# Picking source rows with TensorE from the first step to the last, with the parts of x made between k and v

## The chip, the cores and the metric

The kernel runs on one core of one Trainium2 chip. The metric is device time in microseconds (us) of one launch. The kernel before has a median of 3076.03 us over 14 runs (3071.71 to 3078.97). Profiles come from one execution each, taken by the hardware profiler.

The engines are named as in the profile: PE is TensorE (PEld its weight loads), DVE is VectorE, ACT is ScalarE, POOL is GpSimd, and SP is SyncE, which here only issues DMAs.

## What is computed

The reference is one layer of a graph network with a residual and a layer norm. There are 6,250 nodes with 64 features and 206,250 edges, sorted by destination:

```python
Qh = (x @ Wq.T + bq).reshape(n, H, D)          # H = 4, D = 16
Kh = (x @ Wk.T + bk).reshape(n, H, D)
Vh = (x @ Wv.T + bv).reshape(n, H, D)
Ee = (edge_attr @ We.T + be).reshape(-1, H, D)
score = (Kh[src] * Qh[dst] * (1.0 / np.sqrt(D)) * Ee).sum(-1)
score = jnp.exp(jnp.clip(score, -5.0, 5.0))
msg = Vh[src] * score[..., None]
wV = jax.ops.segment_sum(msg, dst, num_segments=n)
x = _layernorm(x + wV.reshape(n, H * D), axis=-1)
```

Every edge needs the k and v rows of its source (a row of 128 floats at a random place of a table) and the q row of its destination (near its neighbours', since the edges are sorted).

## The kernel before

**Tiling.** 128 edges make a tile, 8 tiles a group, and 202 groups hold the 1,612 tiles. A step works on two groups; the last eight groups are a step each. That makes 105 steps: 0 to 96 with 16 tiles and 97 to 104 with 8 (the last has 4).

**Order.** The program is written out by hand under a manual schedule: each engine runs its instructions in exactly the order in which the source emits them, and waits in that order too.

**Prologue.** k and v of all nodes are computed (L320) and written to a table in HBM. Meanwhile POOL fetches rows of x for the first four groups (L230). Then q is computed in three bf16 parts (L350, L352, L353 and a helper) and written to a second table. Last, a loop over the first four groups in halves turns the fetched x rows (L375, copied by L378) and multiplies them (L380, L382, copied by L384) into k and v of these groups. The xT table (64 features, padded to 6,400 nodes) lies in SBUF for all this. After the prologue POOL has sent 32 gathers for groups 4 to 7; then a branch on a loaded value begins the main path.

**The five buffers.** A step's k and v rows stand in one of five buffers of 16 tiles. Normally a tile's rows come by one indirect DMA from the table (L402, sent by POOL). The gathers for step s + 4 are emitted in step s, behind the message product L619; their buffer is the one that L619 of step s - 1 read last.

**One step s**, in short: squares and relu on ACT make one-hot columns of the destinations for step s + 1 (L555, L572, L577); sums of step s - 1 (L638); products k * q * e (L602, L603), their sum and exponential (L609, L611, L612); the message (L619); its split in three bf16 parts, where PE subtracts between two ACT copies (L622, L630, L632); the one-hot matrix of the next step (L585) and its queries (L595).

**Picking.** For two tiles of most steps the rows aren't gathered. PE picks them instead. The table of x, split in three bf16 parts, lies in SBUF as 50 blocks of 128 rows (`parts`). For a tile, ACT subtracts 50 * column from the source numbers (L466), PE turns that (L471), DVE compares it with the block numbers in two halves of 25 blocks (L481, two "hots" a tile), and PE multiplies each of the 50 one-hot blocks with its block of parts (L491, 50 matmuls a tile). DVE sums the three parts (L498); PE turns the result (L505, copied by L507) and multiplies it by the k and v weights (L513, L515); ACT copies it into the buffer (L516). The pick of step p spans steps p and p + 1 and serves step p + 2, of which it fills the last two tiles. Here p runs from `M0` = 4 to `LAST` = 94: 91 picks, 182 tiles.

**Making the parts.** In steps 0 to 3 the function `table_parts` loads x in seven blocks on SP's queue (L448) and splits it on ACT and DVE (L450, L451, L456 to L458), two blocks a step.

**Row fetches.** Every sixth step from 12 to 96 ("rowed") has one further tile whose rows SP fetches one by one (L544) into a tile that ACT copies (L548).

**Count.** Of the 1,612 tiles, 32 come from the prologue, 182 are picked, 15 are fetched by SP and 1,383 gathered by L402.

Of the kernel before, what the change touches and what calls it, by code (L numbers as in the profile page):

```python
# [37 lines left out]
CB = 10  # L38
KVB = 5
XG = 4  # L40
TB = 8
M0 = 4
PAD = N
SPARE = N + 1
TABLES = 4
# [4 lines left out]
def tiles_of(g):  # L50
    return min(G, T - g * G)
# [9 lines left out]

LAST = NS - 8 - 3


def picks_in(s):
    return M0 <= s <= LAST

# [33 lines left out]
def tile_gnn(ctx: ExitStack, tc: tile.TileContext, x, xT, wT, bias, beT, weT, eT, src, dst, dst_rows,  # L103
# [50 lines left out]
    be_p = consts.tile([3, G, C], BF16, name="be_p")  # L154
    wkv = consts.tile([P, 2, 2 * C], F32, name="wkv")
    bkv_p = consts.tile([3, G // 2, 2 * C], BF16, name="bkv_p")
    minus_b = consts.tile([P, P], BF16, name="minus_b")

    acc = consts.tile([P, RING, 4, C], F32, name="acc")
# [24 lines left out]
    with tc.tile_pool(name="nodes", bufs=1) as nodes, \  # L184
# [182 lines left out]
            fetch_queries(g)  # L367


        for g in range(XG):  # L370
            for h in range(2):
                tp = npsum.tile([P, 2, P], F32, name="tp", bufs=2)
                for u in range(2):
                    j = 4 * h + 2 * u
                    nc.tensor.transpose(tp[:, u, :],  # L375
                                        XS[g][:, j:j + 2, :].rearrange("p j c -> p (j c)"), ident)
                xe = nodes.tile([P, 2, P], F32, name="xe", bufs=2)
                nc.scalar.activation(xe, tp, AF.Copy)  # L378
                pv = npsum.tile([P, 4, 2 * C], F32, name="pv", bufs=2)
                nc.tensor.matmul(pv, ones_b, bkv_p, start=True, stop=False, skip_group_check=True)  # L380
                for u in range(2):
                    nc.tensor.matmul(pv[:, 2 * u:2 * u + 2, :], xe[:, u, :], wkv, start=False,  # L382
                                     stop=u == 1, skip_group_check=True)
                nc.scalar.activation(kv_of(g)[:, 4 * h:4 * h + 4, :], pv, AF.Copy)  # L384

    def edge_values(pe, et, n):

# [6 lines left out]
    def keys(t0):  # L394

        n = min(KEYS, T - t0)
        nc.vector.tensor_scalar(key_i[:, :n], dst_i[:, t0:t0 + n], P - 1, None, op0=OP.bitwise_and)
        nc.vector.tensor_copy(key[:, t0:t0 + n], key_i[:, :n, None].to_broadcast([P, n, 2]))

    def gather_kv(g, j):  # L400
        t = g * G + j
        nc.gpsimd.indirect_dma_start(  # L402
            out=kv_of(g)[:, j, :], out_offset=None, in_=kv_tab[:, :],
            in_offset=bass.IndirectOffsetOnAxis(ap=src_i[:, t:t + 1], axis=0))

    for g in range(XG, 2 * KVB - 2):
        for j in range(G):
            gather_kv(g, j)

    rv = nc.values_load(n_wide[0:1, 0:1], min_val=0, max_val=NR2 * 4)  # L410

    with tc.If(rv == 0) as branch:

        with tc.tile_pool(name="work", bufs=2) as work, \
# [11 lines left out]
            parts = accp.tile([P, NB, 3, C], BF16, name="parts")  # L426
            nc.vector.memset(parts, 0.0)
            NX = N // NB
            x_v = x.rearrange("(p b) c -> p b c", p=NX)
            n_picks = LAST - M0 + 1  # L430
            src_f = accp.tile([P, n_picks, 2], F32, name="src_f")
            t0 = (M0 + 3) * 2 * G - 2
            for i in range(2):
                nc.vector.tensor_copy(src_f[:, :, i],
                                      src_i[:, t0 + i:t0 + i + 2 * G * (n_picks - 1) + 1:2 * G])
            pick = fixed.tile([P, 4 * P], F32, name="pick")
            rows3 = pick[:, :6 * C].rearrange("p (k i c) -> p k i c", k=2, i=3)
            HOT, FAR, X = {}, {}, {}
# [2 lines left out]

                return ap.rearrange("p (a b) -> p a b", b=2)

            def table_parts(b):

                n = min(TB, NB - b)
                raw = work.tile([P, TB, C], F32, name="raw", bufs=1)
                nc.sync.dma_start(raw[:NX, :n], x_v[:, b:b + n, :])  # L448
                rest = pick[:NX, :n * C].rearrange("p (b c) -> p b c", b=n)
                nc.scalar.activation(rest, raw[:NX, :n], AF.Copy)  # L450
                nc.scalar.activation(parts[:NX, b:b + n, 0], raw[:NX, :n], AF.Copy)  # L451
                return rest

            def table_parts_rest(b, rest):
                n = min(TB, NB - b)
                nc.vector.tensor_sub(rest, rest, parts[:NX, b:b + n, 0])  # L456
                nc.scalar.activation(parts[:NX, b:b + n, 1], rest, AF.Copy)
                nc.vector.tensor_sub(parts[:NX, b:b + n, 2], rest, parts[:NX, b:b + n, 1])  # L458

            def sources(s, i):  # L460

                if picks_in(s):
                    FAR[s, i] = work.tile([P, P], BF16, name="far")
                    nc.scalar.activation(FAR[s, i], row50, AF.Identity,  # L466
                                         bias=src_f[:, s - M0, i:i + 1], scale=-1.0)

            def sources_turned(s, i):
                if picks_in(s):  # L470
# [39 lines left out]
            def picked_kv(s):  # L510
                if picks_in(s):
                    xe, kv = X.pop(s)
                    nc.tensor.matmul(kv, ones_b, bkv_p[:, :2], start=True, stop=False,  # L513
                                     skip_group_check=True)
                    nc.tensor.matmul(kv, xe, wkv, start=False, stop=True, skip_group_check=True)  # L515
                    nc.scalar.activation(kvs[(s + 2) % KVB][:, 2 * G - 2:, :], kv, AF.Copy)  # L516

            def gather(s):
                for g in groups_of(s):
                    for j in range(tiles_of(g)):  # L520
                        if is_rowed(s) and (g - STEPS[s][0]) * G + j == COLUMN:
                            continue
                        if not picks_in(s - 2) or g == STEPS[s][0] or j < G - 2:
                            gather_kv(g, j)

            RS, RK = {}, {}
# [53 lines left out]
            def onehot_edges(s):  # L580

                n, t0 = tiles_in(s), STEPS[s][0] * G
                OH[s] = work.tile([P, 2 * G, P], BF16, name="of")
                shape = [P, n, P // 2, 2]
                nc.vector.tensor_tensor(OH[s].rearrange("p t (a c) -> p t a c", c=2)[:, :n],  # L585
                                        pairs(col)[:, None].to_broadcast(shape),
                                        key[:, t0:t0 + n, None, :].to_broadcast(shape),
                                        op=OP.is_equal)
# [109 lines left out]
                                               op0=OP.mult, op1=OP.add)  # L698

            closed, scaled, normed = 0, 0, 0  # L700
            keys(0)
            for k, g in enumerate(groups_of(0)):
                onehot_rows(g, spread(g))
# [1 line left out]
                edges(0, k)  # L705
            queries(0)
            onehot_edges(0)
            for s in range(NS):
                more = s + 1 < NS
                for g in groups_of(s):  # L710
# [9 lines left out]
                    onehot_rows_rest(nexts[0])  # L720
                if s:
                    sums(s - 1)
                sources_turned(s, 1)
                sources_turned(s + 1, 0)
                if nexts[1:]:
                    onehot_rows(nexts[1], spread(nexts[1]))
                making = [b for b in range(s * 2 * TB, (s + 1) * 2 * TB, TB) if b < NB]
                if making:
                    rest = table_parts(making[0])
                prod = products(s)  # L730
                picked(s - 1)
                if more:
                    edges(s + 1, 0)
                picks(s, 0, 0)
# [5 lines left out]
                msg = message(s, score)  # L740
                if s + KVB - 1 < NS:
                    gather(s + KVB - 1)
                picked_turned(s - 1)
                if nexts[1:]:
                    edges(s + 1, 1)
                minus(s, msg, 0)
                hots(s, 1, 0)
                picks(s, 0, 1)
                minus(s, msg, 1)
                picked_kv(s - 1)  # L750
                if not more:

                    close(B - 2)
                    spreads(B - 2)
                hots(s, 1, 1)
                picks(s, 1, 0)
                sources(s + 1, 1)
                sources(s + 2, 0)
                if s + 1 < NS:
                    rows_fetched(s + 1)  # L760
                if more:
# [21 lines left out]
                for i, b in enumerate(making):  # L783
                    if i:
                        rest = table_parts(b)
                    table_parts_rest(b, rest)
            assert normed == B - 2
            sums(NS - 1)
            roots(B - 2, B - 1)
# [9 lines left out]
    with branch.Else():  # L799

        sums = [dram.tile([NR, C], F32, name=f"sums{i}") for i in range(TABLES)]
        with tc.tile_pool(name="gconsts", bufs=1) as gc, \
                tc.tile_pool(name="gloads", bufs=3) as loads, \
                tc.tile_pool(name="ggath", bufs=4) as gath, \
# [28 lines left out]
            def gather(g, j):  # L833
                if j == 0:
                    Q[g] = gath.tile([P, G, C], F32, name="gq")
                t = g * G + j
                if g >= 2 * KVB - 2:
# [125 lines left out]
```

## Time and profile before

| What | us |
|---|---|
| median of 14 runs | 3076.03 |
| the profiled execution | 3077.2 |
| its span, first to last instruction | 3075.2 |
| POOL busy in L402 (1,383 gathers of 0.946) | 1308.5 |
| PE busy in the picks, L491 (9,100 of 0.115 in the mean) | 1046.0 |
| DVE busy in the hots, L481 (364 of 1.818 and a pipelined start) | 651.3 |
| PE waits before the queries, L595, for nothing that the profile shows | 562.7 |
| mean granted TensorE clock | 0.783 |

How to read it: the time of one execution is its span and some 2 us around it. Busy time is an engine's work, not its share of what sets the end; no engine is busy for more than two thirds of the span. "Wait" lines name the waiting engine and line, who released it, the total in us, the count and the longest. "Remote" means that a semaphore changed with no instruction ending just before. A gather's duration is POOL's own work for it; the rows land later. Gathers that follow each other start 1.25 us apart.

### The profile page before, as it was taken

What the parts mean: (1) busy time and instruction counts of PE and PEld (TensorE: products, weight loads), DVE (VectorE), ACT (ScalarE), POOL (GpSimd) and SP (SyncE); (2) the same over time, 40 slices, a digit from 0 to 9 for tenths busy, and PEclk for the clock granted to TensorE, in tenths of its full rate; (3) what the DMA queues carried; (4) which work ended last, traced back from release to release, by engine and by line L of the source; (5) the groups of instructions that cost most, each with busy time, mean ns of one, the idle gap of its engine ahead of it and who ended that gap; (6) DMA issues with size and microseconds to landing.
All of it is one profiled execution on the core that took longest, in us unless ns stands there. A gap on an engine that the chain in (4) does not pass through costs nothing. (4 is left out here: it accounts for less than half of the span.)

```text
span 3075.2 us, 44286 instructions
## 1 busy us (share of the span) xinstructions
PE 1987.2 (65%) x15751; PEld 1552.6 (50%) x15751; DVE 1503.4 (49%) x1695; ACT 918.7 (30%) x1328; POOL 1340.6 (44%) x1427
## 2 busy tenths in 40 slices
PE   4555766657676666667576766666576766667675
PEld 4334545545454555545454555545454545545553
DVE  3234545545454545545454545445454545455554
ACT  2242323323232323223232322323232323223334
POOL 5455444343444444353444444353434444453342
PEclk9967878778787878777777778777777878777885
DMA  5222112121212112221211111121212122121121
GB/s 145 71 77 60 53 45 56 44 58 44 55 45 54 53 46 52 53 58 44 56 51 48 53 46 48 51 57 44 60 46 56 45 54 54 46 58 42 51 58 31
DMA packets 109971, 166.71 MB, mean 54 GB/s; under 512 B 69197, under 2 KB 71453, under 8 KB 109627
## 3 DMA queue, kind: packets, MB, share of 16 engines
q0 software_dynamic: 45280, 91.78, 11.8%
q1 hardware_dynamic: 64074, 71.01, 8.0%
q8 instruction: 125, 2.05, 0.3%
q10 hardware_dynamic: 384, 1.00, 0.2%
q14 instruction: 108, 0.88, 0.1%
HBM read 156.33 MB, written 7.33 MB: 53 GB/s over the span
## 5 line engine op out<-in xcount | busy, mean ns | idle before, releaser
L402 POOL DMA_INDIRECT kv<-kv_tab,src_i x1383 | 1308.5, 946 | 1677.7 <-DVE pq L619 1237.3
L491 PE MATMUL pick<-parts,hot 128*128 128x192 bf16 x9100 | 1046.0, 275 | 267.4 <-issue 266.6
L491 PEld LDWEIGHTS <-hot 128*128 128x128 bf16 x9100 | 889.4, 109 | 398.3 <-issue 342.8
L481 DVE TENSOR_TENSOR hot<-small,block 128x3200 bf16<-128x3200 bf16 x364 | 651.3, 1818 | 298.5 <-remote 258.1
L595 PE MATMUL pq<-qw,to 126*128 126x64 bf16 x1612 | 164.0, 221 | 663.6 <-issue 562.7
L572 ACT ACTIVATE to<-pb,minus_row 126x1024 bf16<-126x1024 f32 x202 | 223.1, 1104 | 996.5 <-PE pb L555 941.5
L602 DVE TENSOR_TENSOR prod<-kv,pq 128x1024 f32<-128x1024 f32 (+2 forms) x105 | 123.7, 1178 | 779.6 <-PE pq L595 387.5
L595 PEld LDWEIGHTS <-to 126*128 126x128 bf16 x1612 | 108.0, 113 | 739.9 <-issue 736.5
L632 ACT ACTIVATE msg<-pq 128x1024 bf16<-128x1024 f32 (+2 forms) x210 | 207.8, 990 | 771.5 <-remote 522.6
L391 PE MATMUL pe<-we_sb,et 128*128 128x128 f32 x1612 | 247.6, 299 | 0.0
L391 PEld LDWEIGHTS pe<-we_sb,et 128*128 128x128 f32 x1612 | 207.3, 201 | 54.1 <-issue 48.3
L577 ACT ACTIVATE to<-to,one_p 126x1024 bf16<-126x1024 bf16 x202 | 230.6, 1142 | 3.5
L609 DVE TENSOR_REDUCE small<-prod 128x64 f32<-128x1024 f32 (+2 forms) x105 | 124.4, 1185 | 188.1 <-PE small L471 148.3
L638 PEld LDWEIGHTS <-of 128*128 128x128 bf16 x1612 | 156.6, 108 | 49.9 <-issue 41.0
L638 PE MATMUL small<-msg,of 128*128 128x192 bf16 x1612 | 170.9, 265 | 0.5 <-ACT msg L632 0.5
L630 PE MATMUL pq<-msg,minus_b 128*128 128x512 bf16 x404 | 128.5, 398 | 59.0 <-ACT msg L622 45.3
L555 PE MATMUL pb<-key_rows,ident_b 112*128 112x512 bf16 x403 | 154.2, 472 | 4.9 <-ACT to L572 2.6
L622 ACT ACTIVATE msg<-pq 128x1024 bf16<-128x1024 f32 (+2 forms) x105 | 103.9, 990 | 95.9 <-DVE pq L619 95.9
L603 DVE TENSOR_TENSOR prod<-prod,pe 128x1024 f32<-128x1024 f32 (+2 forms) x105 | 123.6, 1177 | 3.6
L619 DVE TENSOR_TENSOR pq<-kv,small 128x1024 f32<-128x1024 f32 (+2 forms) x105 | 123.5, 1176 | 1.4 <-ACT small L612 1.4
L585 DVE TENSOR_TENSOR of<-small,key 128x2048 bf16<-128x2048 bf16 (+2 forms) x105 | 123.2, 1173 | 0.3
L498 DVE TENSOR_REDUCE xp<-pick 128x128 f32<-128x384 f32 x91 | 50.7, 558 | 98.8 <-PE pick L491 98.3
(129 smaller groups left out, 992.1 us busy)
## 6 DMA issues: line engine op xcount, KB each, us to landing
et<-in_eT SPq DMA_DIRECT2D x100, 512.0 KB
rk<-kv_tab SPq DMA_DIRECT2D x1920, 0.5 KB
kv<-kv_tab,src_i POOLq DMA_INDIRECT x1383
qw<-q_tab SPq DMA_DIRECT2D x202, 15.8 KB
kv_tab<-kv_sb SPq DMA_DIRECT2D x5, 640.0 KB
q_tab<-q SPq DMA_DIRECT2D x5, 480.0 KB
acc<-in_x SPq DMA_DIRECT2D x48, 32.0 KB
out<-y SPq DMA_DIRECT2D x48, 32.0 KB
```

Of the source, the lines that this page charges most:

```text
L391: nc.tensor.matmul(pe[:, 2 * u:2 * u + 2, :], et[:, u, :], we_sb, start=False, stop=u == n // 2 - 1, skip_group_check=True)
L402: nc.gpsimd.indirect_dma_start(out=kv_of(g)[:, j, :], out_offset=None, in_=kv_tab[:, :], in_offset=bass.IndirectOffsetOnAxis(ap=src_i[:, t ...
L481: nc.vector.tensor_tensor(HOT[s, i, h].rearrange("p b (a c) -> p b a c", c=2), pairs(from_b[i])[:, None].to_broadcast(shape), block2[:, bl ...
L491: nc.tensor.matmul(rows3[:, i], hot[:, k, :], parts[:, b], start=b == 0, stop=b == NB - 1)
L555: nc.tensor.matmul(pb[:, b:b + 4, :], ident_b[:NR2, g // 2:g // 2 + 1].to_broadcast([NR2, P]), key_rows[:, g % 2, b * P:(b + 4) * P], star ...
L572: nc.scalar.activation(TO[g][:, :n, :], pb[:3 * W, :n, :], AF.Square, bias=minus_row3[:3 * W])
L577: nc.scalar.activation(TO[g][:, :n, :], TO[g][:, :n, :], AF.Relu, bias=one_p[:3 * W], scale=-1.0)
L595: nc.tensor.matmul(PQ[s][:, (g - STEPS[s][0]) * G + j, :], TO[g][:, j, :], QW[g], start=j == 0, stop=j == tiles_of(g) - 1, skip_group_chec ...
L609: nc.vector.tensor_reduce(score, prod[:, :n, :].rearrange("p g (h d) -> p g h d", h=H), axis=AX.X, op=OP.add)
L630: nc.tensor.matmul(msg[:, lo:hi, :], minus_b, M3[s][:, lo:hi, i, :], start=False, stop=True, skip_group_check=True)
L632: nc.scalar.activation(M3[s][:, :n, i + 1, :], msg[:, :n, :], AF.Copy)
L638: nc.tensor.matmul(PA[s], OH[s][:, j, :], M3[s][:, j], start=j == 0, stop=j == n - 1)
```

## The change

The parts of x are now made in the prologue, out of the xT table in SBUF, by PE transposes between the turned x rows and the k and v of the first groups. No step makes parts any more, and the loads of x for them and the memset are gone. Picks run from step 0 on (`PAIRS`, `TARGET`): steps 0 to 96 pick two tiles each for the step two later. Picks 97, 99 and 101 are spread over two steps each, one tile in each step, and serve steps 100, 102 and 104, each a step of one group, whose last two tiles they fill. So 200 tiles are to be picked, and L402's gathers go down by 18. Step 0's first hots are made before the loop.

The core of the diff:

```diff
-TB = 8
-M0 = 4
+TB = 4
-LAST = NS - 8 - 3
-def picks_in(s):
-    return M0 <= s <= LAST
+LAST = NS - 8 - 1
+PAIRS = [*range(LAST + 1), *range(LAST + 1, NS - 3, 2)]
+TARGET = {p: p + (2 if p <= LAST else 3) for p in PAIRS}
+def picks_in(p):
+    return p in PAIRS
+def second_of(s):
+    return s if s <= LAST else s - 1 if s - 1 in PAIRS else None
+def is_picked(g, j):
+    s = max(s for s in range(NS) if STEPS[s][0] <= g)
+    return s in TARGET.values() and g == groups_of(s)[-1] and j >= tiles_of(g) - 2
...
+        def parts_of_x(b):
+            n = min(TB, NB - b)
+            px = npsum.tile([P, 2, 2 * C], F32, name="ps").rearrange("p i (j c) -> p (i j) c", j=2)
+            px = px[:, :n]
+            for u in range(n):
+                nc.tensor.transpose(px[:, u, :], xT_sb[:C, (b + u) * P:(b + u + 1) * P],
+                                    ident[:C, :C])
+            nc.scalar.activation(parts[:, b:b + n, 0], px, AF.Copy)
+            nc.vector.tensor_sub(px, px, parts[:, b:b + n, 0])
+            halves.append((px, b, n))
+        def rest_of_x():
+            px, b, n = halves.pop(0)
+            nc.scalar.activation(parts[:, b:b + n, 1], px, AF.Copy)
+            nc.vector.tensor_sub(parts[:, b:b + n, 2], px, parts[:, b:b + n, 1])
+        order = [(g, h) for g in range(XG) for h in range(2)]
+        blocks = list(range(0, NB, TB))
+        xe = x_turned(*order[0])
+        for i, gh in enumerate(order):
+            following = x_turned(*order[i + 1]) if i + 1 < len(order) else None
+            for b in blocks[2 * i:2 * i + 2]:
+                parts_of_x(b)
+            first_kv(*gh, xe)
+            xe = following
+            while halves:
+                rest_of_x()
...
     for g in range(XG, 2 * KVB - 2):
         for j in range(G):
-            gather_kv(g, j)
+            if not is_picked(g, j):
+                gather_kv(g, j)
...
-                    nc.scalar.activation(kvs[(s + 2) % KVB][:, 2 * G - 2:, :], kv, AF.Copy)
+                    n = tiles_in(TARGET[s])
+                    nc.scalar.activation(kvs[TARGET[s] % KVB][:, n - 2:n, :], kv, AF.Copy)
...
+            sources(0, 0)
+            sources_turned(0, 0)
             keys(0)
...
             onehot_edges(0)
+            sources(0, 1)
+            sources(1, 0)
+            for h in range(2):
+                hots(0, 0, h)
             for s in range(NS):
...
-                sources_turned(s, 1)
+                sources_turned(second_of(s), 1)
                 sources_turned(s + 1, 0)
...
-                making = [b for b in range(s * 2 * TB, (s + 1) * 2 * TB, TB) if b < NB]
-                if making:
-                    rest = table_parts(making[0])
                 prod = products(s)
-                picked(s - 1)
+                picked(second_of(s - 1))
...
-                picked_turned(s - 1)
+                picked_turned(second_of(s - 1))
...
-                hots(s, 1, 0)
+                hots(second_of(s), 1, 0)
                 picks(s, 0, 1)
                 minus(s, msg, 1)
-                picked_kv(s - 1)
+                picked_kv(second_of(s - 1))
...
-                hots(s, 1, 1)
-                picks(s, 1, 0)
-                sources(s + 1, 1)
+                hots(second_of(s), 1, 1)
+                picks(second_of(s), 1, 0)
+                sources(second_of(s + 1), 1)
...
-                picks(s, 1, 1)
+                picks(second_of(s), 1, 1)
```

`x_turned(g, h)` and `first_kv(g, h, xe)` are the two halves of the old loop over the first groups, unchanged. The rest of the diff sets `src_f` (the source numbers of the picked tiles) for all picks, removes `table_parts`, and lets the other branch, which doesn't run here, gather the tiles that are now left out ahead of it.

More of the change, by code (lines that the diff above doesn't have):

```diff
@@ L156, in tile_gnn @@
     bkv_p = consts.tile([3, G // 2, 2 * C], BF16, name="bkv_p")
+    parts = consts.tile([P, NB, 3, C], BF16, name="parts")
     minus_b = consts.tile([P, P], BF16, name="minus_b")
@@ L367, in tile_gnn, with x_turned @@
             fetch_queries(g)
[L370 to L384, printed above, removed]
+        def x_turned(g, h):
+            tp = npsum.tile([P, 2, P], F32, name="tp", bufs=2)
+            for u in range(2):
+                j = 4 * h + 2 * u
+                nc.tensor.transpose(tp[:, u, :], XS[g][:, j:j + 2, :].rearrange("p j c -> p (j c)"),
+                                    ident)
+            xe = nodes.tile([P, 2, P], F32, name="xe", bufs=2)
+            nc.scalar.activation(xe, tp, AF.Copy)
+            return xe
@@ new lines, in first_kv @@
+        def first_kv(g, h, xe):
+            pv = npsum.tile([P, 4, 2 * C], F32, name="pv", bufs=2)
+            nc.tensor.matmul(pv, ones_b, bkv_p, start=True, stop=False, skip_group_check=True)
+            for u in range(2):
+                nc.tensor.matmul(pv[:, 2 * u:2 * u + 2, :], xe[:, u, :], wkv, start=False,
+                                 stop=u == 1, skip_group_check=True)
+            nc.scalar.activation(kv_of(g)[:, 4 * h:4 * h + 4, :], pv, AF.Copy)
+        halves = []
+        def parts_of_x(b):
[8 more added lines that the diff above has]
+            halves.append((px, b, n))
@@ L424, in tile_gnn @@
             nc.tensor.transpose(col, row_b[:, 0:1].to_broadcast([P, P]), ident_b)
[L426 to L432, printed above, removed]
-            for i in range(2):
-                nc.vector.tensor_copy(src_f[:, :, i],
-                                      src_i[:, t0 + i:t0 + i + 2 * G * (n_picks - 1) + 1:2 * G])
+            src_f = accp.tile([P, PAIRS[-1] + 1, 2], F32, name="src_f")
+            full = NS - 8 - 2
+            for i in range(2):
+                t0 = 3 * 2 * G - 2 + i
+                nc.vector.tensor_copy(src_f[:, :full, i],
+                                      src_i[:, t0:t0 + 2 * G * (full - 1) + 1:2 * G])
+            for p in PAIRS[full:]:
+                t0 = STEPS[TARGET[p]][0] * G + tiles_in(TARGET[p]) - 2
+                nc.vector.tensor_copy(src_f[:, p], src_i[:, t0:t0 + 2])
             pick = fixed.tile([P, 4 * P], F32, name="pick")
@@ L442, in pairs @@
                 return ap.rearrange("p (a b) -> p a b", b=2)
[L444 to L458, printed above, removed]
             def sources(s, i):
@@ L466, in sources @@
                     nc.scalar.activation(FAR[s, i], row50, AF.Identity,
-                                         bias=src_f[:, s - M0, i:i + 1], scale=-1.0)
+                                         bias=src_f[:, s, i:i + 1], scale=-1.0)
             def sources_turned(s, i):
@@ L522, in gather @@
                             continue
-                        if not picks_in(s - 2) or g == STEPS[s][0] or j < G - 2:
+                        if not is_picked(g, j):
                             gather_kv(g, j)
@@ L782, in tile_gnn @@
                             normed += 1
[L783 to L786, printed above, removed]
             assert normed == B - 2
@@ L803, in tile_gnn @@
                 tc.tile_pool(name="gloads", bufs=3) as loads, \
-                tc.tile_pool(name="ggath", bufs=4) as gath, \
+                tc.tile_pool(name="ggath", bufs=3) as gath, \
                 tc.tile_pool(name="gwork", bufs=2) as work, \
@@ L836, in gather @@
                 t = g * G + j
-                if g >= 2 * KVB - 2:
+                if g >= 2 * KVB - 2 or is_picked(g, j):
                     gather_kv(g, j)
```

## The prediction

> **What bounds the kernel now.** I read the wait table first, since no engine is busy for more than 65% of the span.
>
> ```profile
> PE 1987.2 (65%) x15751; PEld 1552.6 (50%) x15751; DVE 1503.4 (49%) x1695; ACT 918.7 (30%) x1328; POOL 1340.6 (44%) x1427
> ...
> POOL kv L402 <- DVE pq L619: 1237.3, 98, 14.6
> ACT msg L632 <- remote: 522.6, 53, 15.8
> DVE hot L481 <- remote: 258.1, 50, 9.6
> ```
>
> Two things are to be seen. POOL's row gathers (L402) idle 1237.3 us until the message product L619 of a step frees a kv buffer: each step sends one burst of gathers right behind its L619. And ACT and DVE wait long for a semaphore that no instruction ended just before ("remote"): what they wait for is PE. The timeline of one step, at 1004 us, shows why (start, duration, engine, line; in brackets the idle time before and what ended it).
>
> ```profile
> 1004.09 0.95 POOL L402 DMA_INDIRECT kv<-kv_tab,src_i  x1 [12.76 <-DVE pq L619]
> ...
> 1007.88 0.59 PE L630 MATMUL pq<-msg,minus_b 128*128 128x512 bf16 x2
> ...
> 1016.85 1.02 ACT L632 ACTIVATE msg<-pq 128x1024 bf16<-128x1024 f32 x1 [9.81 <-remote]
> ...
> 1020.36 0.94 POOL L402 DMA_INDIRECT kv<-kv_tab,src_i  x1 [0.30 <-issue]
> ...
> 1024.33 4.19 PE L491 MATMUL pick<-parts,hot 128*128 128x192 bf16 x25
> 1024.61 1.22 DVE L602 TENSOR_TENSOR prod<-kv,pq 128x1024 f32<-128x1024 f32 x1 [6.62 <-PE pq L595]
> ...
> 1035.00 0.94 POOL L402 DMA_INDIRECT kv<-kv_tab,src_i  x1 [13.70 <-DVE pq L619]
> ```
>
> PE's L630 is recorded at 1007.88, yet ACT, which needs it alone, starts at 1016.85. While the 14 gathers run (17.2 us) PE crawls; the work left over, 13.70 us from the burst's end to the next, sets the step: 17.2 + 13.7 = 30.9. So a step is worth its burst plus whatever PE, DVE and ACT still have to do behind it. That second part I read from a table by stage, cut at the starts of L619 (width, busy us of PE, PEld, DVE, ACT, POOL, then clock, DMA share, GB/s).
>
> ```profile
> 181.40:205.95 24.55, 12.58 (x58) 7.94 (x58) 9.60 (x14) 11.20 (x15) 13.23 (x14) 0.50 0.30 81
> 229.50:253.00 23.50, 12.85 (x77) 8.42 (x76) 11.83 (x17) 8.57 (x12) 13.23 (x14) 0.65 0.26 65
> 283.20:313.80 30.60, 19.59 (x167) 15.70 (x165) 15.44 (x19) 8.62 (x13) 13.24 (x14) 0.78 0.19 50
> 2921.60:2945.50 23.90, 19.39 (x167) 15.47 (x165) 14.45 (x14) 8.22 (x12) 7.58 (x8) 0.86 0.17 47
> 2966.80:2982.10 15.30, 8.80 (x58) 5.87 (x58) 6.85 (x9) 6.68 (x10) 7.56 (x8) 0.78 0.26 70
> 3031.90:3040.40 8.50, 6.37 (x30) 3.80 (x30) 4.81 (x12) 4.24 (x6) 0.00 (x0) 0.50 0.07 15
> ```
>
> With 14 gathers, a step without picking takes 23.5 to 24.6 and one with it 30.6. With 8 gathers they take 15.3 and 23.9. So **picking costs 6 to 8.6 us in a step**, and a gather less saves (30.6 - 23.9)/6 = 1.1 us. Two tiles picked save 2.2 and cost three times that. The change adds picking to the stages that are cheap now.
>
> **The prologue.** Removed from the first four steps: seven loads on SP's queue, the memset of the parts, and the making with 35 short instructions (five for each of seven blocks); in step 0 two of them (L450, L451, 0.59 + 0.62) stand before the exponential on ACT: -1.1. Added between k and v: 50 transposes on PE, 26 copies on ACT (some 0.38 each, by L378's 128x256) and 26 DVE subtractions. The loop there is PE's alone:
>
> ```profile
> 113.37 2.79 PE L350 MATMUL ps<-w_sb,xT_sb 65*128 65x64 f32 x12 [2.44 <-DVE q L341]
> ...
> 119.32 0.63 PE L375 MATMUL tp<-ident,xs 128*128 128x128 f32 x2
> 119.89 0.60 PE L380 MATMUL pv<-bkv_p,ones_b 3*128 3x512 bf16 x1
> 120.49 2.07 PE L382 MATMUL pv<-wkv,xe 128*128 128x256 f32 x4
> ```
>
> Eight rounds of 3.0 us, PE without a gap, so the transposes add their whole time; ACT and DVE, with under 3 us a round, hide behind. A transpose of 64 columns lies between a 64-wide float matmul pass (2.79/12 = 0.23) and a 128-wide transpose (0.63/2 = 0.32): I take 0.27, 50 of them 13.5. If PE left idle time they would cost nothing; it leaves none. The next to be late is step 0, whose spreads stand behind the loop on PE. Against this, the burst at 67 to 107 us has 28 gathers in place of 32. The q matmuls (L350) crawl under it and run freely again only at 112: -4 x 1.25 = -5.0. The two new hots and the first FAR before step 0 lie behind the 4.06 us that the memset (L427) frees on DVE. Sum: 13.5 - 5.0 - 1.1 = **+7.4**; from 0 (transposes at 0.23, half of them in gaps) to +27, if the transposes, which read xT_sb as L350 does, crawl as it did for the 20 us of the burst that runs beside the loop.
>
> **The first four steps.** From L619 of step 0 to that of step 4 the trace has 26.7 + 24.5 + 23.6 + 23.5 = 98.3. Each becomes a picking step: four L481 of 1.82 on DVE, 100 pairs on PE, the reduction L498 between the products and the scores (its 0.56 and a wait for the last pick, 98.3/82 = 1.2, with L609 queued behind), two L466 and L507, L516 on ACT with the next step's squares (L572) queued behind. Rather than add these, I take what a step with all of them lasts, 30.1 (L619 of step 4 starts at 253.0, of step 91 at 2870.2: 2617.2/87): 4 x 30.1 - 98.3 = **+22.1**. Bounds: -2.5 (all hidden, and two gathers less in the first burst), +26 (31.1, the longest usual step). I stay with the steady row, since step 4, the first that picks, already takes 30.2 under the same loads.
>
> **The last steps.** L619 of steps 92 to 100 starts at 2897.7, 2921.6, 2945.5, 2966.8, 2982.1, 2995.1, 3003.7, 3023.3 and 3031.9, then every 8.6 us. Bursts for steps 97 and 98 lose two gathers: 2 x -2.2. Step 95 begins to pick, so the period before its L619 becomes 23.9 in place of 21.3 (+2.6). The next two, 15.4 and 13.0, become picking periods: + 8.6 - 2.2 and + 8.6. Then come single-group steps of 8.6. Picks 97, 99 and 101 spread over two steps each, 50 pairs a step, half of 8.6: 4.3 for each of steps 99 to 102. One oddity: for step 97 the function second_of returns 96, which was finished in step 96, so tile two of 96 is picked **again**, and its reduction and kv again in step 98; the instruction order of the changed kernel has 10,050 pick matmuls where 100 pairs of tiles need 10,000. So step 97 does a whole pick, +8.6. Step 98 has half a pick, but its 19.6 hold a stall behind 16 gathers in a row (the products at 3018.63 idled 7.37), which longer steps spread: +2. Sum: -4.4 + 2.6 + 6.4 + 8.6 + 8.6 + 2 + 17.2 = **+41**. Bounds: +15 if the half picks fit into PE's idle time (8.5 - 6.4 = 2.1 a step), +55 if each costs as much as a half at the low clock: 50 pairs of 4.19/25 = 8.4.
>
> The row 25 pairs in 4.19 has a twin of 2.23 at 1001.81, at granted clocks of 0.50 and 1.00; the tail stands at 0.50. The Trainium skill, TensorE: Matmul & The Clock Gate (Part 1: The HAM clock gate), has the clock full after some 3.4 us of dense work and half after an idle window: by it the picks warm the tail, and an estimate is 4.5 in place of 8.4 a half step.
>
> **Sum:** 7.4 + 22.1 + 41 = 70.5 on the span of 3075.2: 3146; the profiled run, 3077.2 with what lies around, lies 1.2 over the median 3076.0. Forecast **3146**.
>
> **Rivals.** (1) *The prologue crawls* under the burst: +20, 3166. For it: L350's groups of four took 9 us there; against: L375 to L382 ran under a burst without a delay. (2) *Half picks hide* in the short steps, 41 becomes 15: 3120. For: PE has idle time there; against: a picking step's DVE and PE order puts hots and picks between L619 and the products. (3) *Bursts alone decide*, picks are free: each gather less is worth 1.25 us of POOL; four of the 18 are in the prologue's sum, so 3076 + 7.4 - 14 x 1.25 = 3066, **faster**. It decides if a pick leaves under 2.5 us behind its burst. For: picks overlap the burst in part, and rare 13-gather steps last 27.5, 3 us less than those of 14. Against: 23.5 beside 30.6 at equal gathers. The Trainium skill, SBUF — State Buffer (Who interferes with whom), says that DMA never contends with a compute engine and that PE waits on no one; by it PE would not crawl, and a pick's cost would be its 100 pairs alone. The row at 1016.85 differs, and the row decides. (4) *The change does not do what it says:* the repeat of 96 is such a case and is in the sum; without it 3137.
>
> **How the numbers follow.** Forecast 0.65, rival 1 0.15, rival 2 0.13, rival 3 0.05, and 0.02 that it comes out level. All but the last two are slower: 0.93. 0.2%, some 6 us, is what a measurement here tells from no change. The range reaches down to a free prologue with first steps and tail of +15 each, 3076 + 30 = 3106, and up to a crawling prologue (27) with first steps of 24 and a tail of 50: 3177.
>
> **What would show it.** L619 of step 0 near 162 in place of 154.7; then four periods near 30; steady periods unchanged; periods of about 21 before step 97, 13 after it; clock above 0.5 in the tail. Wrong if the first four periods stay under 27, or the single-group steps stay near 9.

## The result, and the profile after

The changed kernel takes 3112.71 us (median of 6 runs, 3107.48 to 3119.07) against 3076.69 for the kernel before in the same comparison: ratio 1.0116, 95% interval 1.0106 to 1.0126. It is 36 us slower; the forecast was 70 us slower (3146), so the sign and the range held, and the forecast rise was about twice the measured one. The profiled execution has a span of 3111.0, 35.8 more than before.

Where the 35.8 went is read from the table by stage. The first fence is the kernel before, the second the changed one; both are cut at the starts of the message product (L619 before, L650 after) of steps 0, 4 and 91. Columns: stretch, width, busy us of PE, PEld, DVE, ACT and POOL (with instructions), granted clock, DMA share, GB/s.

```profile
0.00:154.75 154.75, 83.17 (x311) 64.93 (x311) 46.15 (x134) 37.98 (x103) 77.53 (x92) 1.00 0.37 107
154.75:253.00 98.25, 50.76 (x262) 32.95 (x261) 40.11 (x51) 41.43 (x55) 54.85 (x58) 0.63 0.28 76
253.00:2870.20 2617.20, 1719.74 (x14252) 1359.58 (x14252) 1311.98 (x1348) 761.52 (x1063) 1139.15 (x1204) 0.78 0.19 51
```

```profile
0.00:156.41 156.41, 88.76 (x360) 70.14 (x361) 55.51 (x165) 45.53 (x130) 71.88 (x86) 1.00 0.36 105
156.41:275.40 118.99, 81.08 (x671) 64.42 (x671) 58.22 (x55) 34.72 (x47) 52.84 (x56) 0.80 0.18 46
275.40:2892.69 2617.29, 1721.35 (x14269) 1363.43 (x14267) 1312.11 (x1348) 761.88 (x1065) 1136.23 (x1204) 0.78 0.19 51
```

What remains to the end is 3075.2 - 2870.2 = 205.0 before and 3111.0 - 2892.7 = 218.3 after. So:

| Stage | predicted | measured |
|---|---|---|
| prologue, to the message of step 0 | +7.4 | +1.7 |
| first four steps | +22.1 | +20.7 |
| steady steps 4 to 90 | 0 | +0.1 |
| step 91 to the end | +41 | +13.3 |
| sum | +70.5 | +35.8 |

The wait table of the changed kernel (waiting engine and line, released by what; total, count, longest; three of its lines) has the same two signs as before: POOL waits for the message, and ACT and DVE wait for a PE whose recorded work ended long ago.

```profile
POOL kv L448 <- DVE pq L650: 1280.7, 99, 22.7
...
ACT msg L663 <- remote: 555.1, 58, 13.7
...
DVE hot L511 <- remote: 271.4, 53, 10.9
```

**The prologue** in the timeline, two lines of the kernel before (the first and the last matmuls of its loop):

```profile
116.22 0.69 PE L375 MATMUL tp<-ident,xs 128*128 128x128 f32 x2
...
138.69 2.07 PE L382 MATMUL pv<-wkv,xe 128*128 128x256 f32 x4
```

and the same places of the changed kernel, with the new transposes between them:

```profile
110.05 1.12 PE L388 MATMUL tp<-ident,xs 128*128 128x128 f32 x4
...
111.09 1.11 PE L409 MATMUL ps<-ident,xT_sb 64*128 64x64 f32 x8
...
115.11 1.11 PE L409 MATMUL ps<-ident,xT_sb 64*128 64x64 f32 x8
...
140.22 2.08 PE L398 MATMUL pv<-wkv,xe 128*128 128x256 f32 x4
```

The loop begins 6.2 us earlier, behind a burst that has four gathers less (5.0 was predicted). Eight transposes take 1.11, so one takes 0.139 where the prediction took 0.27; a round goes from 3.03 to 4.01. The loop lasts 32.3 in place of 24.5; some 1.5 of these 7.7 us are idle time of PE around the last two transposes (136.51, below), not the transposes' own. From the loop's end to the message it is 14.1 in place of 14.0: -6.17 + 7.71 + 0.12 = +1.66.

Behind the loop two changes cancel. The message of step 0 no longer waits for the two copies that made parts on ACT, but PE's first step work (L586) starts 1.88 us behind the loop in place of 0.74, since the first FAR and its transpose now stand ahead of it:

```profile
136.51 0.45 PE L409 MATMUL ps<-ident,xT_sb 64*128 64x64 f32 x2 [1.27 <-issue]
...
143.64 0.40 ACT L496 ACTIVATE far<-row,src_f 128x128 bf16<-128x128 f32 x1 [0.71 <-DVE key_i L443]
144.10 0.29 PE L501 MATMUL small<-ident_b,far 128*128 128x128 bf16 x1 [0.86 <-ACT far L496]
144.18 1.06 PE L586 MATMUL pb<-key_rows,ident_b 112*128 112x512 bf16 x2
```

**The tail** by steps 92, 93, 94, 97, 99, 100 and 101, cut at L650 (same columns):

```profile
2920.38:2938.94 18.56, 16.12 (x167) 13.41 (x165) 15.21 (x17) 8.54 (x13) 5.67 (x6) 1.00 0.20 53
2938.94:2959.04 20.10, 17.70 (x167) 14.78 (x165) 14.48 (x14) 8.53 (x13) 5.66 (x6) 0.92 0.19 49
2959.04:2981.28 22.24, 18.82 (x164) 15.58 (x162) 15.30 (x17) 8.64 (x13) 7.56 (x8) 0.85 0.18 49
...
3017.10:3032.19 15.09, 12.54 (x130) 10.73 (x128) 8.23 (x13) 5.31 (x10) 5.66 (x6) 1.00 0.24 64
...
3049.20:3058.24 9.04, 7.73 (x73) 5.97 (x71) 4.89 (x13) 5.27 (x10) 1.88 (x2) 1.00 0.19 54
3058.24:3071.70 13.46, 11.41 (x94) 9.66 (x94) 12.17 (x18) 4.14 (x6) 0.00 (x0) 0.75 0.05 10
3071.70:3080.73 9.03, 7.65 (x72) 5.86 (x70) 4.87 (x12) 4.98 (x9) 0.00 (x0) 1.00 0.07 15
```

Three things are to be seen. Steps 92 and 93, with 6 gathers in place of 8, last 18.6 and 20.1 in place of 23.9 and 23.9: a gather less is worth 1.9 to 2.7 us here, not 1.1. In the kernel before, in the step of the prediction's timeline whose burst begins at 1004.09, PE first pauses for nothing that the profile shows 7.1 us into the burst:

```profile
1011.18 0.34 PE L491 MATMUL pick<-parts,hot 128*128 128x192 bf16 x2 [0.48 <-issue]
```

Six gathers last 7.2 us and eight 9.7, so a burst of six is over about when PE begins to fall behind. That fits the gain; no run tests it by itself.

Second, the granted clock is 0.75 to 1.00 in steps 97 and 99 to 101, where before it was 0.50 to 0.54 from step 97 on. The eight edge matmuls of such a step, before and after:

```profile
3038.97 2.08 PE L391 MATMUL pe<-we_sb,et 128*128 128x128 f32 x8
...
3056.30 1.16 PE L437 MATMUL pe<-we_sb,et 128*128 128x128 f32 x8
```

At full clock a step with half a pick takes 9.03, hardly more than a step without one at half clock (8.56). Third, steps 99 and 101 make no hots; step 100 makes four, and DVE is busy for 12.2 of its 13.5 us.

### The profile page after: what moved, and what is told of

It is laid out like the page before. It is cut to its first block, busy times and chain, and to the rows that moved or that the text cites. A ratio compares the mean times of both kernels' runs of the same rounds, so it can differ in the third digit from the quotient of the medians.

```text
span 3111.0 us, 46506 instructions
## 1 busy us (share of the span) xinstructions
PE 2061.3 (66%) x16810; PEld 1636.7 (53%) x16810; DVE 1571.8 (51%) x1759; ACT 926.0 (30%) x1372; POOL 1320.4 (42%) x1409
## 5 line engine op out<-in xcount | busy, mean ns | idle before, releaser
L448 POOL DMA_INDIRECT kv<-kv_tab,src_i x1365 | 1288.1, 944 | 1721.2 <-DVE pq L650 1280.7
L521 PE MATMUL pick<-parts,hot 128*128 128x192 bf16 x10050 | 1141.3, 274 | 292.0 <-issue 291.3
L521 PEld LDWEIGHTS <-hot 128*128 128x128 bf16 x10050 | 976.8, 109 | 429.9 <-issue 367.7
L511 DVE TENSOR_TENSOR hot<-small,block 128x3200 bf16<-128x3200 bf16 x402 | 718.8, 1817 | 293.8 <-remote 271.4
L663 ACT ACTIVATE msg<-pq 128x1024 bf16<-128x1024 f32 (+2 forms) x210 | 207.6, 989 | 768.8 <-remote 555.1
L437 PE MATMUL pe<-we_sb,et 128*128 128x128 f32 x1612 | 236.9, 291 | 0.0
L437 PEld LDWEIGHTS pe<-we_sb,et 128*128 128x128 f32 x1612 | 198.0, 193 | 46.3 <-issue 43.0
L586 PE MATMUL pb<-key_rows,ident_b 112*128 112x512 bf16 x403 | 148.8, 457 | 1.5 <-ACT to L603 1.0
L650 DVE TENSOR_TENSOR pq<-kv,small 128x1024 f32<-128x1024 f32 (+2 forms) x105 | 123.5, 1176 | 0.3 <-ACT small L643 0.3
```

Of the source, the lines that this page charges most:

```text
L437: nc.tensor.matmul(pe[:, 2 * u:2 * u + 2, :], et[:, u, :], we_sb, start=False, stop=u == n // 2 - 1, skip_group_check=True)
L448: nc.gpsimd.indirect_dma_start(out=kv_of(g)[:, j, :], out_offset=None, in_=kv_tab[:, :], in_offset=bass.IndirectOffsetOnAxis(ap=src_i[:, t ...
L511: nc.vector.tensor_tensor(HOT[s, i, h].rearrange("p b (a c) -> p b a c", c=2), pairs(from_b[i])[:, None].to_broadcast(shape), block2[:, bl ...
L521: nc.tensor.matmul(rows3[:, i], hot[:, k, :], parts[:, b], start=b == 0, stop=b == NB - 1)
L586: nc.tensor.matmul(pb[:, b:b + 4, :], ident_b[:NR2, g // 2:g // 2 + 1].to_broadcast([NR2, P]), key_rows[:, g % 2, b * P:(b + 4) * P], star ...
L663: nc.scalar.activation(M3[s][:, :n, i + 1, :], msg[:, :n, :], AF.Copy)
```

## The experiments

Each kernel is compared with the kernel before on the same chip. The runs went to four chips, and this matters: on chips 13 and 15 the kernel before takes 3095 and 3096 us, on chips 0 and 3 it takes 1790 and 1793. Ratios, not times, are compared between chips of one kind. The unaltered changed kernel did not run on chip 13; e4, which differs from it by 2 to 4 us in one step, is the nearest there.

### e1: no picks at all

```diff
-PAIRS = [*range(LAST + 1), *range(LAST + 1, NS - 3, 2)]
+PAIRS = []
...
-            for b in blocks[2 * i:2 * i + 2]:
-                parts_of_x(b)
```

> No tile is picked and no parts are made: 1,565 gathers instead of 1,365, no hots, no picks. Theory: a step lasts its burst of gathers plus what PE, DVE and ACT still do behind it, 6.9 us without picking and 13.7 with it (rows of the kernel before). A step of 16 gathers then lasts 20.0 + 6.7 = 26.7 in place of 30.1, as step 0 of the kernel before did (26.66), a step with 15 about 25.4; 87 steady steps save some 87 x 3.6 = 310 us, the first four and the tail some 20 more: about 2780 us. Rival 'bursts alone decide': 200 gathers more at 1.25 us make it slower than after, 3113 + 250 = 3360. A middle result (near 3000) would mean that a longer burst holds PE back by more than its 1.25 us a gather.

Measured on chip 13: 2758.21 us, ratio 0.8914 (0.8899 to 0.8929). Two of its steps in the table by stage, cut at its message product:

```profile
281.25:308.02 26.77, 13.05 (x58) 8.00 (x58) 7.88 (x13) 7.70 (x9) 15.09 (x16) 0.56 0.21 62
1716.24:1743.06 26.82, 12.71 (x58) 7.71 (x58) 7.89 (x14) 7.91 (x10) 15.10 (x16) 0.56 0.21 61
```

Sixteen gathers and 26.8 us, the 26.7 of "burst plus 6.7". This is the reasoning of the prediction tested far from where it was read: picking two tiles costs 30.1 - 26.7 = 3.4 us a step more than gathering them (3.6 by the means of steps 4 to 90 on this chip, 26.6 here and 30.2 in e3). The rival "bursts alone decide" (3360) is out on this chip.

### e2, e3, e4: one part of the change undone

e2 gathers the tiles that steps 0 to 3 would pick, e3 those of the picks from 95 on, e4 picks the second tile of 96 once:

```diff
-PAIRS = [*range(LAST + 1), *range(LAST + 1, NS - 3, 2)]
+PAIRS = [*range(4, LAST + 1), *range(LAST + 1, NS - 3, 2)]     # e2
+PAIRS = [*range(LAST - 1)]                                     # e3
...
-    return s if s <= LAST else s - 1 if s - 1 in PAIRS else None
+    return s if s <= LAST else s - 1 if s - 1 > LAST and s - 1 in PAIRS else None   # e4
```

> The changed kernel with the picks of steps 0 to 3 left out (their 8 tiles are gathered), all else as in after. Stage theory: the first four steps cost 119.0 us in after and 98.3 before, so undoing them gives back 20 us or a little more, since nothing makes parts in them now: 3113 - 21 = 3092, range 3085 to 3096. Rival 'the loss sits elsewhere and is only seen here' (parts in the prologue delay the first steps through queues): 3108 to 3113.

Measured on chip 13: ratio 1.0069 (1.0053 to 1.0086). From after's 1.0116 that is 0.47% or 14.5 us (12.6 against e4 on the same chip), less than the 20 expected and outside the range that was given. The table by stage of e2, cut at L650 of steps 0 and 4, shows both halves of it:

```profile
0.00:163.05 163.05, 88.36 (x357) 69.88 (x358) 52.24 (x164) 44.30 (x127) 77.34 (x92) 1.00 0.34 104
163.05:260.46 97.41, 50.56 (x265) 33.01 (x265) 31.76 (x37) 32.27 (x36) 54.73 (x58) 0.61 0.20 57
```

In e3 and e4, on the same chip, step 0 reaches its message at 159.80 and 158.44, and the four steps last 120.0 and 120.3. So four steps without picks save 22.7, and with the four gathers that come back into the prologue the message comes 3.3 to 4.6 later. The expectation had left those out. The rest of the shortfall sits where the edit changes nothing: from step 4 to 91 e2's trace has 2635.6 us and e4's 2632.0, and behind that 221.8 and 216.5. That part is not explained by the stage theory.

> The changed kernel with picks 95, 96, 97, 99 and 101 left out (their ten tiles are gathered). Stage theory: from L650 of step 91 to the end after lasts 218.3 us and before 205.0, so undoing gives back 13.4: 3113 - 13 = 3099.5, range 3096 to 3102. Rival of the prediction (the tail costs 41): 3072.

Measured on chip 13: ratio 1.0084 (1.0067 to 1.0100), 0.32% or 10 us below after, a little less than the 13 expected. From L650 of step 91 to the end e3 has 206.7 us, against 216.5 in e4 and 218.3 in after. The stage theory holds; the 41 of the prediction does not. Steps 92 and 93 of e3, with 8 gathers again, last 23.5 and 23.7; those of e4, with 6, 20.2 and 18.6: the gain of the shorter bursts is seen on this chip too. The same last steps as in after took 221.8 us in e2 and 219.8 in e9, so 2 or 3 us in a single trace carry little.

> The changed kernel with the second tile of step 96 picked once (step 97 does half a pick, step 98 none of the sums, turns and products of it). The prediction's theory: the repeat costs +8.6 in step 97 and up to 2 behind it: 3104. Trace theory: steps 96 to 98 last 18.88, 15.09 and 17.01 in after against 13.00, 8.56, 19.63 before, +9.8 together, of which half a pick in step 97 must stay; half of step 97's +6.5 goes: 3109.5. Rival 'repeat hidden': 3113, no change.

Measured on chip 13: ratio 1.0117 (1.0100 to 1.0134): no difference from after that this can tell. In its trace step 97 lasts 13.04 in place of 15.09 (15.2 in e2, 16.7 in e9). By the traces the repeated pick of 96 costs 2 to 4 us, not the 8.6 to 10.6 of the expectation's first theory; the total can't tell it from nothing.

### e5 to e8: rests between the gathers

What holds PE back during a burst? Three theories: PE lives on a store of instructions that fills only between gathers; PE needs a fixed time without gathers; gathers simply take time in proportion. Short iotas on POOL, which write a tile that nothing reads, make rests; e5 to e7 are e1 with them, e8 is the changed kernel with them.

```diff
+            sent = [0]
+            idle = accp.tile([P, 512], I32, name="idle")
...
             def gather(s):
+                sent[0] = 0
...
                             gather_kv(g, j)
+                            sent[0] += 1
+                            if s < NS - 8 and sent[0] % 8 == 0:      # e6: 4, e7 and e8: 1
+                                for _ in range(4):                  # e6, e7 and e8: 1
+                                    nc.gpsimd.iota(idle, pattern=[[1, 512]], base=0,    # e7, e8: 256
+                                                   channel_multiplier=0)
```

> e1 (no picks), and in each step of two groups POOL rests after 8 and after 16 gathers: four iotas of 512 numbers, an estimate of 2 to 3 us (the 224-wide iota took 0.32). In e1 a step is 26.75 us: 20.0 of gathers and 6.75 behind them. Theory 'store': PE has some 55 instructions in store when a burst begins, which are done after 3 us (the trace of after), and then hardly any reach it until the burst ends; a rest fills the store again. Then work for 55 instructions moves from behind the burst into it: 20 + 2.5 + some 3 behind = 25 to 26 a step, 2758 - 97 x 1.2 = about 2640 to 2700. Theory 'silence': PE needs its 6.75 us without gathers anywhere: the rest counts as part of them, no change, 2750 to 2770. Theory 'proportion': rests only delay the gathers: + 2.5 a rest in the middle of each step, 2758 + 97 x 2.5 = 3000.

> e1, with one iota of 512 numbers (an estimate of 0.6 us) after every fourth gather. 'Store', if a rest of 0.6 us is long enough for the store to fill: three refills of 55 instructions cover all that a step without picking has (some 120): 20 + 2 + 1 to 2 behind it = 23 to 24, about 2450. 'Silence': 2750 to 2770. 'Proportion': 2758 + 97 x 1.8 = 2930.

> e1, with an iota of 256 numbers (an estimate of 0.35 us) after every gather, so that the same rest is spread finest: 16 x 0.35 = 5.6 us a step. 'Store': if a rest of 0.35 us lets ten or more instructions through, PE is never held and the step is the gathers with their rests, 16 x 1.6 = 25.6 or less: about 2650; if such a rest is too short to let any through, 26.75 + 5.6 = 32.3: about 3290. 'Silence': the 5.6 count, 2750 to 2770. 'Proportion': 3290.

> The changed kernel itself with the same iota of 256 after every gather of the steps of two groups. A step is 17.2 + 13.0 = 30.1 us there; it has some 330 PE instructions. 'Store' with rests that let instructions through: 14 x 1.6 = 22.4 of gathers, under which PE goes on, so that a step is 23 to 26 us: 2550 to 2750 in all. Rests too short, or 'proportion': 14 x 0.35 = 4.9 a step more, about 3590. 'Silence': 3110 to 3130.

Measured: 2419.33, 2175.63, 2362.77 and 2102.41 us, ratios 1.3515, 1.2154, 1.3201 and 1.1751. They tell nothing about the three theories, because they ran on chip 0, where the kernel before takes 1789.95 us. There PE isn't held back: in the wait table of e8 no engine waits for "remote" at all, where after has 555.1, 271.4, 197.8 and 126.6 us in its four largest such lines. With PE free, POOL sends gather after gather, and rests only lengthen that row (proportion). So the comparison up to here holds for one kind of chip only.

### e9 and e10: the changed kernel again, and five stretches in one kernel

> The changed kernel once more, unaltered, beside the kernel before on this call's chip. Runs e5 to e8 had a chip on which the kernel before takes 1790 us in place of 3076 to 3095. There 1,383 gathers of 1.25 us make 1729 us, so that POOL's gathers would be the bound, and the third rival of the prediction ('bursts alone decide') would hold: 18 gathers less are worth 22 us, ratio 0.987 (0.98 to 0.995). On a chip on which the kernel before takes some 3080 us, picking costs 3.4 us a step more than gathering its tiles, and the ratio is that of the first comparison, 1.011 to 1.013.

Measured on chip 15: 3135.85 against 3095.91 us, ratio 1.0130 (1.0113 to 1.0147). The first comparison holds on another chip of the kind that takes some 3080 us for the kernel before.

e10 puts the rests into one kernel so that either kind of chip answers:

```diff
-PAIRS = [*range(LAST + 1), *range(LAST + 1, NS - 3, 2)]
+PAIRS = [*range(61), *range(LAST - 1, LAST + 1), *range(LAST + 1, NS - 3, 2)]
...
+            def rest(s, k):
+                n = (256 if 27 <= s < 46 else
+                     2048 if 46 <= s < 65 and k == 7 else
+                     512 if 65 <= s < 83 and k % 4 == 0 else 0)
+                if n:
+                    nc.gpsimd.iota(idle[:, :n], pattern=[[1, n]], base=0, channel_multiplier=0)
```

> One kernel with five stretches (numbers of the steps that hold them fully): A, steps 6 to 20, as in after; B, 24 to 38, an iota of 256 after each gather (0.36 us of POOL, a gather and its rest took 1.48 in e8); C, 43 to 55, one iota of 2,048 numbers (some 2 us) after the seventh gather; D, 63 to 76, no picks and an iota of 512 (0.57 us) after each fourth of 16 gathers; E, 80 to 90, no picks and no rests. Steps on a chip where the kernel before takes some 3080 us: A 30.1 and E 26.7 by every theory. 'Store' (PE's store of instructions fills in each rest): B 22 to 26, C 27 to 28.5, D 21.8 to 24. 'Silence' (rests count toward the 13.0 or 6.7 us that PE needs without gathers): B 30.1, C 30.1, D 26.7. 'Proportion' (rests only delay): B 33.5, C 32.2, D 28.5. On a chip where it takes 1790 us PE isn't held, and every stretch is POOL's gathers with their rests: A 17.3, B 20.7, C 19.5, D 21.7 (as in e6), E 20.0.

Measured on chip 15: 2889.21 us, ratio 0.9332 (0.9313 to 0.9351). The table by stage of e10, cut at its message product so that the rows are the stretches A to E (15, 15, 13, 14 and 11 steps):

```profile
345.16:796.78 451.62, 292.46 (x2465) 233.94 (x2463) 224.44 (x227) 130.01 (x183) 195.48 (x207) 0.78 0.17 50
880.69:1277.29 396.60, 312.06 (x2462) 232.91 (x2462) 229.96 (x250) 133.21 (x186) 269.86 (x414) 0.86 0.20 59
1384.49:1738.44 353.95, 272.42 (x2125) 212.45 (x2123) 193.91 (x196) 113.54 (x159) 193.12 (x192) 0.82 0.19 56
1938.26:2310.18 371.92, 145.48 (x812) 92.59 (x812) 108.13 (x162) 110.40 (x118) 240.64 (x276) 0.61 0.22 63
2388.73:2682.13 293.40, 133.04 (x638) 83.84 (x638) 81.27 (x110) 85.19 (x91) 165.27 (x175) 0.57 0.21 61
```

Divided by their steps: A 30.1, B 26.4, C 27.2, D 26.6, E 26.7. In B and C POOL does more than in A (the same gathers and the rests), and the step is 3.7 and 2.9 us **shorter**. "Proportion" (33.5 and 32.2) and "silence" (30.1) fall there; "store" (22 to 26 and 27 to 28.5) is met in C and missed by 0.4 in B. The timeline of a step of C shows what the rest does (start, duration, engine, line; in brackets the idle time before and what ended it):

```profile
1498.40 0.94 POOL L448 DMA_INDIRECT kv<-kv_tab,src_i  x1 [0.30 <-issue]
1499.35 1.85 POOL L567 IOTA idle<- 128x2048 int32 x1
1500.29 1.02 ACT L675 ACTIVATE msg<-pq 128x1024 bf16<-128x1024 f32 x1 [6.95 <-remote]
1501.20 1.82 DVE L513 TENSOR_TENSOR hot<-small,block 128x3200 bf16<-128x3200 bf16 x1 [4.24 <-remote]
```

Seven gathers are sent; ACT has waited 6.95 us for a PE subtraction and DVE 4.24 us for a hot that picks must free, and within the 1.85 us of the rest both go on. D says otherwise: rests of 0.57 gain nothing there (26.6, the 26.7 of "silence", where "store" had 21.8 to 24).

```profile
2092.86 0.94 POOL L448 DMA_INDIRECT kv<-kv_tab,src_i  x1 [0.30 <-issue]
2093.81 0.57 POOL L567 IOTA idle<- 128x512 int32 x1
2094.37 1.23 DVE L652 TENSOR_REDUCE small<-prod 128x64 f32<-128x1024 f32 x1 [11.88 <-remote]
```

The score reduction of D stood still through two earlier rests of this burst and went on only when it was over. A rest must be long enough, it seems; but B's many rests of 0.36 do help. So it is shown that the rests of B and C let work on PE go on; by what rule is open, and none of the three theories meets B, C and D.

### e11 and e12: the other kind of chip

> The changed kernel, unaltered, on this call's chip. Where the kernel before takes some 3080 us: ratio 1.011 to 1.013, as twice so far. Where it takes 1790 us, PE isn't held during bursts and POOL's gathers are the bound (1,383 of 1.25 us are 1729 us of 1790): 18 gathers less are worth 22 us, ratio 0.987 (0.98 to 0.995), and the change makes the kernel faster.

> The kernel of e5, unaltered: no picks, and four iotas of 512 (0.57 us each, 2.3 us together) after 8 and after 16 gathers. It took 2419 us on a chip that runs the kernel before in 1790 us; there 2419 again. On a chip of 3080 us: 'store' says that a rest of over 1.8 us, after which the lag of PE ended in stretch C of e10, fills PE's store, so that two stores of 42 to 68 instructions meet the step's 120: 20.0 + 2.3 + 1 to 3 = 23.3 to 25.3 in place of 26.75, 2420 to 2620 in all; 'silence' (the rest counts toward the 6.75 us): 26.75, as e1, 2758, and so no gain, as in stretch D; 'proportion': 29, 2980.

Measured on chip 3: 1803.19 against 1793.34 us, ratio 1.0061 (1.0044 to 1.0078), for the changed kernel; 2423.81, ratio 1.3516, for e12, as on chip 0. The expected gain of 22 us isn't there: the change is 10 us slower on this chip too. The wait table of e11:

```profile
ACT to L603 <- PE pb L586: 400.0, 105, 6.4
POOL kv L448 <- issue: 392.7, 1288, 0.3
```

POOL waits for no one any more, only the 0.3 us between gathers, and no line of the table names "remote". The table by stage for e11, a stretch of ten early steps and the one from the last gather's end to the end:

```profile
158.27:315.89 157.62, 157.15 (x1643) 134.35 (x1641) 147.53 (x153) 85.95 (x122) 119.21 (x127) 1.00 0.34 91
...
1747.35:1797.48 50.13, 32.59 (x260) 25.49 (x259) 30.09 (x61) 16.89 (x32) 0.00 (x0) 0.74 0.05 11
```

and the stretch behind the last gather for e12:

```profile
2403.14:2421.71 18.57, 4.48 (x21) 2.17 (x19) 7.01 (x23) 4.80 (x10) 0.00 (x0) 0.50 0.05 11
```

Ten picking steps, 4 to 13, last 157.6 us with PE busy for 157.2 of them: here PE is the bound as soon as POOL isn't. All 1,397 gathers of the program are sent by 1747.35, one every 1.249 us; the kernel before has 18 more and would send its last near 1770. What is left then is 50.1 us with picks in the tail and 18.6 without (e12). -22.5 + 31.5 = +9.0, and +9.85 was measured. The kernel before has no trace on this chip, so its two numbers are worked out, and the 18.6 is that of a kernel without any picks; a change that leaves the picks 95 to 101 out was not tried there. That the gain is lost in the tail is therefore argued, not shown.

## Why the prediction was right, and where its size was off

- **A step is its burst plus what PE has left behind it.** Right on the kind of chip of the result: on chip 13 e1, with 16 gathers and no picks, gives the 26.8 us that the rule asks for. On chips 0 and 3 the premise, a PE that crawls while gathers run, isn't there. What makes PE crawl was not predicted and stays open.
- **First four steps, +22.1.** Measured 20.7, and 22.7 by e2 against e3 and e4. The steady row was the right choice.
- **Prologue, +7.4.** "I take 0.27" is the step that was mis-sized: the 64-wide transpose takes 0.139, below the 0.23 of the lower neighbour that the bound used, so the loop grew by 7.7 in place of 13.5. The four gathers were near their price (-6.2 for -5.0; 3.3 to 4.6 by e2), and rival 1, the crawl, didn't come. The -1.1 for the copies on ACT came, but the first FAR, which the prediction put at nothing behind the memset's time, holds PE back by 1.1, so the two cancel (+0.1).
- **Last steps, +41.** Here lies the miss, 28 us of the 35. Four terms of the sum were too high. (a) The two bursts with two gathers less were put at -2.2 each by the slope of 1.1; steps 92 and 93 gave -5.3 and -3.8. (b) "+ 8.6 - 2.2 and + 8.6" for the two periods that become picking ones, 95 and 96, were +1.6 and +5.9, and the step ahead of them +1.0 for +2.6. (c) "Step 97 does a whole pick, +8.6", then "+2": steps 97 and 98 gave +6.5 and -2.6, and e4 puts the repeat itself at 2 to 4. The 3137 that rival 4 has without the repeat takes 9 off, more than the sum holds for it: half of step 97's 8.6 is the first half of pick 97. (d) "50 pairs a step, half of 8.6" in four steps: 17.2 was 0.5, 4.9, 0.5 and 3.5, together 9.3; the two large ones are the steps in which DVE makes four hots, which the prediction spread evenly. Steps 92 to 98, (a) to (c), came to +3.2 for +23.8, so they hold 20.6 of the miss, and the half picks 7.9; the other steps took 0.8 more than before, which the sum had at nothing.
- What (b) to (d) have in common is that a pick was priced by the difference between two steps, as a pure addition. In the tail the clock for everything else changed with the picks. The table has 0.75 to 1.00 in steps 99 to 101 where the kernel before has 0.50; eight edge matmuls take 1.16 in place of 2.08 us, and 25 pairs 2.7 in the mean (345 of them keep PE busy for 37.2 us from 3017 to 3092), where the bound of the prediction had 4.19. How much of the miss the clock explains no run separates: it always rose together with the picks, and in step 92 with a shorter burst. The Trainium skill, TensorE: Matmul & The Clock Gate (Part 1: The HAM clock gate), has the clock rise to full after dense work and fall to half after idle time; the prediction cited it and left it out of the sum. The rows agree with it.
- **Rival 2** (the tail at 15, 3120 us) was the nearest to what came, by luck. Its 15 doesn't follow from its ground: half picks at no cost take 17.2 from the 41 and leave 23.8. What came has the half picks at 9.3, hidden only in steps 99 and 101, and steps 92 to 98 at 3.2, which rival 2 doesn't speak of.
- **Rival 3** needs a chip without the crawl, and even there the changed kernel was 10 us slower; by the working under e11 the freed gathers are lost to the tail.
- Of the signs named beforehand: steady periods unchanged (2617.3 and 2617.2), four periods near 30 (30.7, 29.5, 29.7, 29.1) and a clock above 0.5 in the tail were right; 162 for the first message (156.4) and periods of 21 before step 97 (16.9 to 22.2) were not. Periods of 13 after it came in two of the four half-pick steps (13.5 and 11.3); the other two stayed at 9.0, which the prediction had named as a sign of being wrong, and there it was.

**A version that beats both** on chip 13 is e1, without picks: 0.8914 of the kernel before. It isn't one for every chip. Where the kernel before takes 1790 us, e1's 1,597 gathers of 1.249 us would alone need 1995 (worked out; e1 itself did not run there). Stretch B of e10, picks with rests, is as short a step (26.4) on chip 15; a whole kernel of that kind was run only on chip 0 (e8).

## What to carry to other kernels

Price a piece of work by a kernel in which it is missing, as e1 does for the steady steps and e3 for the tail, before adding up differences of single steps: the steps of a tail differ from steady ones in their clock and in the length of their bursts, and the sum inherits that. When an engine waits for "remote" far behind the recorded end of the instruction it needs, ask first whether this is the kernel or the chip, and compare with a second chip before building a rule on it. And when one engine's work is cut, look at what remains after its last instruction: by the working under e11, 22 us of gathers saved were lost there.

## What the runs showed of the hardware

- **Chips differ by a factor of 1.7 on one program.** The kernel before took 3095 and 3096 us on chips 13 and 15 and 1790 and 1793 on chips 0 and 3. On the first kind ACT and DVE wait for a PE that lags through each burst of gathers (lines "remote", up to 13.7 us at a time in the changed kernel); on the second no such line exists in any of the six traces. Each chip was used at one time only, so that the chip, and not something else of that time, makes the difference is not shown. Why it is so stays open.
- The Trainium skill, SBUF — State Buffer (Who interferes with whom), says of the ports of SBUF that "DMA never contends with a compute engine" and that "PE and ACT never wait on anyone". On chips 0 and 3 no wait in the traces speaks against it. On chips 13 and 15 something does hold PE while gathers run: in stretch C waits of 6.95 and 4.24 us end within a rest in the gathers. Whether that is at the ports of SBUF, of which the page speaks, or elsewhere, no run shows.
- On the first kind **more POOL work made a step shorter**: an iota of 0.36 us behind each of 14 gathers turned 30.1 us into 26.4 (A and B of e10).
- Eight float transposes of 64 columns in a row took 1.11 us, 0.139 each, and made a round of the loop 0.98 longer.
